# Routing the last group of a mixture-of-experts layer in two segments

## The chip, the cores and the metric

The kernel runs on one core of a Trainium2 chip. The metric is the device time of one execution in microseconds (us), and the smaller the better. A core has five engines that run side by side, each through its own queue of instructions in a fixed order: TensorE (PE, matrix products; PEld is its loading of weights), VectorE (DVE), ScalarE (ACT), GpSimd (POOL) and SyncE (SP). Transfers between the chip's main memory and the on-chip memory run on 16 DMA engines; an instruction on SP, ACT or POOL only issues one. An engine waits on semaphores: an instruction that waits holds up everything behind it in its queue.

## The reference

The program is a four-layer network on 2708 nodes with 256 features. Each layer adds a graph step and a feed-forward step to x. The change touches the feed-forward step of layer 1, a mixture of 8 experts in which each node goes to one:

```python
def _L1_ffn_ref(x, W1, b1, Wg, bg, Wd, bd):
    H = gelu(x @ W1 + b1)                      # 2708 x 1024
    probs = softmax(H @ Wg + bg)               # 2708 x 8
    assign = argmax(probs)
    for e in range(8):
        y = H @ Wd[e] + bd[e]                  # 1024 -> 256
        out = out + where(assign == e, probs[:, e] * y, 0)
```

All data are float32. How many nodes each expert gets depends on the data.

## The kernel before

**Tiles and groups.** The 2708 rows are 22 tiles of 128 rows (the last has 20). In layer 1 the graph step runs in three groups of tiles (GROUPS1): 0 to 7, 8 to 15 and 16 to 21. Once a group's graph step is done, `send1` works on its tiles: it normalizes them, makes the hidden rows H in pairs of tiles (L362 products, L364 Gelu on ACT), the gate's logits (L1085, L1092), turns H back into rows (L1102 on DVE) and writes it to a table `hid` in main memory (L1108, L1111; POOL issues these for the first two groups, ACT for the last one). After all pairs of the group come the softmax (ACT changes its function table for the exponential, then about a dozen short DVE instructions) and `route`.

**Routing.** `route` counts with products of the 0/1 choices (L389, L391), how many rows each expert has so far, and gives each row a place in a list `taken` (in main memory) that is sorted by expert within the group. `scatter` then writes one record (row number and probability) for each row, one POOL transfer for each tile (L497, taken). The records stand in a tile `names` with a single buffer; a POOL copy fills in the row numbers (L1115), so the copy for the next group has to wait until the scatters of the one before have read it.

**Blocks.** An expert's rows are worked on in blocks of 128. `blocks` computes on DVE, from the counts, for each block its expert (`b_ei`) and the places of its records (`b_ix`). After two groups 9 blocks can be sure to be full whatever the data (A blocks: 2048 rows in 8 experts leave at most 127 over in each); their list is made after group two. After the last group the rest is listed (B blocks), 21 at most, of which 15 always run (ALWAYS) and 6 stand in a branch that is taken only if the data need more than 24 blocks in all.

**One block.** `Units` runs the blocks as a pipeline. For each block POOL issues three indirect transfers: the gather of its 128 records (L511, names; call it the names gather), the gather of its 128 hidden rows of 4 KB each (L648, hs; the row gather), and at its end the scatter of its result (L497, given). SP issues the load of its expert's weights (L1025, wb, 1152 KB), whose address is read from `b_ei`. PE turns the rows (8 transposes, L659, call it the turn; two ACT copies L660 follow) and multiplies (L698, the product, 16 records in the trace for each block); DVE adds the bias and scales (L699, L700). There are three buffers for rows, three for weights and two for results. `more` fetches up to four names tiles and three row tiles ahead, so that a new row gather waits for a turn to free a buffer.

**Order.** Each engine's order is laid out when the program is built, by a scheduler that goes by dependencies and estimated times. It moves the hidden layer of the last group in between the A blocks' products: PE begins the A blocks when the graph step ends, at 933 us, and works on both until 1014.7. The B blocks follow. A transfer that reads rows which were scattered (`past`) waits for those scatters.

Of the kernel before, what the change touches and what calls it, by code (L numbers as in the profile page):

```python
# [8 lines left out]
F32 = mybir.dt.float32  # L9
# [3 lines left out]
ALU = mybir.AluOpType  # L13
AX = mybir.AxisListType

P = 128
N = 2708
D = 256
DC = D // P
E = 8  # L20
# [9 lines left out]
GROUPS1 = [range(0, 8), range(8, 16), range(16, NT)]  # L30
# [6 lines left out]
def rows(t):  # L37
    return min(P, N - t * P)
# [28 lines left out]
def adj_ffn4(ctx: ExitStack, tc: tile.TileContext, a: dict, out: bass.AP):  # L67
    nc = tc.nc
    v, s, g, te = nc.vector, nc.scalar, nc.gpsimd, nc.tensor
# [340 lines left out]
    def blocks(pool, brief, known, NB, B, name, done=None, full=False, least=0):  # L410
# [12 lines left out]
        vec = pool.tile([P, K, E], F32, name="b_vec", tag="b_vec" + name)  # L423
# [12 lines left out]
        rest = cnt  # L436
        if done is not None:
            rest = pool.tile([P, E], F32, name="b_rest")
# [6 lines left out]
        nb = pool.tile([P, E, 1], F32, name="b_nb")  # L445
# [9 lines left out]
        ei = pool.tile([P, NB], I32, name="b_ei", tag="b_ei" + name)  # L455
        v.tensor_scalar(ei, eb[:, :, 0], float(E - 1), None, op0=ALU.min)
        v.tensor_tensor(vec[:, 0, :], nb[:, :, 0], end, ALU.subtract)
        if done is not None:
            v.tensor_tensor(vec[:, 0, :], vec[:, 0, :], done, ALU.add)
        v.tensor_tensor(hot, eb.to_broadcast([P, NB, E]),  # L460
                        count[:, None, :E].to_broadcast([P, NB, E]), ALU.is_equal)
        part = brief.tile([P, NB, K, E], F32, name="b_part", tag="b_part" + name, bufs=1)
# [17 lines left out]
                            ALU.mult)  # L480
            v.tensor_tensor(ix if full and i == len(known) - 2 else row, row, step, ALU.add)
        if full:

            took = pool.tile([P, E], F32, name="b_took")
            v.tensor_scalar(took, vec[:, 0, :], float(NB), None, op0=ALU.add)
            v.scalar_tensor_tensor(took, took, 0.0, nb[:, :, 0], op0=ALU.max, op1=ALU.min)
            return ei, ix, took
        v.tensor_tensor(step, pos, of[:, :, K - 1 : K].to_broadcast([P, NB, M]), ALU.is_ge)
        v.scalar_tensor_tensor(ix, step, 1e7, row, op0=ALU.mult, op1=ALU.add)
# [2 lines left out]
    scattered = {}  # L492
# [126 lines left out]
    class Units(Blocks):  # L619
# [43 lines left out]
        def begin(self, items):  # L663
# [3 lines left out]
            self.rows_todo = len(items)  # L667
            self.more(False)

        def more(self, weights=True):  # L670
            while self.names_todo and len(self.named) + len(self.rows) < 4:
                self.fetch_names(self.names_todo.pop(0))
            while self.rows_todo and len(self.rows) < 3:
                self.fetch_rows()
                self.rows_todo -= 1
            while weights and self.todo and len(self.ahead) < 2:
                self.fetch(self.todo.pop(0))

        def run(self, pool, items, during=None):
            self.names_todo += items  # L680
            self.todo += items
            self.rows_todo += len(items)
            self.more()
            turned = self.turn(pool, self.rows[0][1])
            n = 0
            while self.rows:
                w2, hT = self.ahead.pop(0), turned
                m, _ = self.rows.pop(0)
                self.more()
                if during is not None:  # L690
                    during(n)
                n += 1
                if self.rows:
                    turned = self.turn(pool, self.rows[0][1])
                y = pool.tile([P, D], F32, name="ys", bufs=2)
                q = pools["psum"].tile([P, W], F32, name="yacc", bufs=2)[:, :D]
                for f in range(HC):
                    te.matmul(q, lhsT=hT[:, f, :], rhs=w2[:, f, :], start=(f == 0), stop=(f == HC - 1))  # L698
                v.tensor_tensor(y, q, w2[:, HC, :], ALU.add)  # L699
                v.tensor_scalar(y, y, m[:, 1:2], None, op0=ALU.mult)  # L700
                scatter(self.given, m[:, 0:1].bitcast(I32), y, self.given.shape[0] - 1, self.ok)
# [309 lines left out]
    held = sum(rows(t) for q in GROUPS1[:-1] for t in q)  # L1011
    NA, MOST = 9, (N - E) // P + E + 1
    assert NA <= -(-(held - E * (P - 1)) // P)
    ALWAYS = 15
    with ExitStack() as l1:
        tp = l1.enter_context(tc.tile_pool(name="t1", reuse_waits="tile", bufs=1))
        w1 = mat(tp, "L1_ffn_W1", 1024)
# [46 lines left out]
        def send1(tiles):  # L1064
# [7 lines left out]
            for i0 in range(0, G, 2):  # L1072
                own = [(i, (i - i0) * P, rows(tiles[i])) for i in range(i0, min(i0 + 2, G))]
                w = own[-1][1] + own[-1][2]
                xT = gt.tile([P, DC, 2 * P], F32, name="xT4", bufs=2)
                for i, k, r in own:
                    xn = work.tile([P, D], F32, name="xn")[:r]
                    norm_to(xn, tiles[i], i, st)
                    turn_to(xT[:, :, k : k + r], xn, r)
                hT = gt.tile([P, HC, 2 * P], F32, name="hT", bufs=1)  # L1080
                hidden(hT, xT, w1, lambda f: b1[:, f : f + 1], 0, w, HC)
                p = ps_tmp()
                for f in range(HC):
                    q = f % 4 * Q
                    te.matmul(p[q : q + Q, :w], lhsT=wg[:, f, :], rhs=hT[:, f, :w],  # L1085
                              start=(f < 4), stop=(f >= HC - 4), tile_position=(0, q))
                lT = gt.tile([P, 2 * P], F32, name="lT", bufs=1)
                s.copy(lT[:, :w], p[:, :w])
                p = ps_tmp()
                for i, k, r in own:  # L1090
                    o = p[:r, (i - i0) * E : (i - i0 + 1) * E]
                    te.matmul(o, lhsT=lT[:, k : k + r], rhs=fold[:, :E], start=True, stop=True)  # L1092
                    v.tensor_tensor(lg[:r, i, :], o, bg[:r], ALU.add)

                queue = s if tiles is GROUPS1[-1] else g
                for i, k, r in own:
                    h = gt.tile([P, P // Q, HC * Q], F32, name="hrow", bufs=2)
                    n = -(-r // Q)
                    if r < P:
                        v.memset(hT[:, :, k + r : k + n * Q], 0.0)  # L1100
                    for f in range(0, HC, 4):
                        v.transpose(h[:, :n, f * Q : (f + 4) * Q].rearrange("p b (f i) -> p f b i", i=Q),  # L1102
                                    hT[:, f : f + 4, k : k + n * Q].rearrange(
                                        "p f (b j) -> p f b j", j=Q))
                    for q in range(P // Q):
                        dst = hid[tiles[i] * P : tiles[i] * P + r, q * HC * Q : (q + 1) * HC * Q]
                        if r == P:
                            queue.dma_start(dst.rearrange("(b j) c -> j b c", j=Q),  # L1108
                                            h[q * Q : (q + 1) * Q])
                        else:  # L1110
                            queue.dma_start(dst, h[q * Q : q * Q + r, 0, :])  # L1111
# [17 lines left out]
        for tiles in GROUPS1:  # L1129
# [66 lines left out]
            if end:  # L1196
# [5 lines left out]
                hc = l1.enter_context(  # L1202
                    tc.tile_pool(name="c1", side="right", reuse_waits="tile", bufs=1))
                work1.more()
            send1(tiles)
            if tiles is GROUPS1[-2]:
                full = blocks(hw, gt, known, NA, P, "A", full=True)
        rest = blocks(hw, gt, known, MOST - NA, P, "B", done=full[2])
        too_many = count_left(hw, (rest[2], ALWAYS))
        gate.close()  # L1210
        past = list(scattered["taken1"])
        items = [(rest, b, past, taken[1], False) for b in range(ALWAYS)]
        more = [(rest, b, past, taken[1], False) for b in range(ALWAYS, MOST - NA)]
        left = []

        def beside(b):
# [693 lines left out]
```

## Time and profile before

| | us |
|---|---|
| median of 3 runs | 1943.4 (1940.89 to 1946.63) |
| profiled execution | 1943.77 |
| its span | 1941.9 |
| PE busy | 1830.7 (94%) |
| DVE, ACT, POOL busy | 1090.2, 666.7, 347.4 |
| A blocks, first turn to last product | 933.4 to 1014.7 |
| B blocks, first turn to last product | 1029.6 to 1102.35 |
| first instruction of layer 2 that needs the result (x on DVE) | 1111.9 |

Times are counted from the start of the span. A busy time is the sum over an engine's instructions; a PE that is busy is not necessarily at its peak. In a list of instructions each row has its start, its length, the engine, the line of the code, the operation, the tiles written and read, and in brackets how long the engine stood idle before it and what it seems to have waited for. In the stretches each engine has its busy time and its number of instructions.

### The profile page before, as it was taken

To read this page: it belongs to the slowest core of one execution; us is meant where nothing else is said; L and a number is where in the kernel's file an instruction comes from. 1 tells how busy PE (TensorE), PEld (TensorE's weight loads), DVE (VectorE), ACT (ScalarE), POOL (GpSimd) and SP (SyncE) were. 2 spreads that over 40 slices of the span, in tenths; PEclk is the share of its full clock that TensorE was granted. 3 is DMA by queue.
4 is the path that set the end of the run, shared out by engine and by line. 5 is a ranking of instruction groups with operands and counts; after the bars stand their busy time and mean duration, and the time that the engine had idled before them with its cause. 6 is when DMAs were issued, how large, how long until landed. Compare 5 with 4: busy or idle time off the path is not lost.

```text
span 1941.9 us, 25771 instructions
## 1 busy us (share of the span) xinstructions
PE 1830.7 (94%) x9441; PEld 1332.3 (69%) x9441; DVE 1090.2 (56%) x2463; ACT 666.7 (34%) x1527; POOL 347.4 (18%) x405
## 2 busy tenths in 40 slices
PE   7999989999999999999887699999899999999997
PEld 6888778888888888887676578888566632232343
DVE  6776862443334434354431265555355499899895
ACT  7868732222223203022222252222243551131232
POOL 1004263333331002213436300000000000000000
PEclk9999989999998999999898899999899999999998
DMA  8435476877764443636768620000101001000000
GB/s 272 137 111 156 121 272 244 346 303 290 296 257 132 146 148 109 159 105 137 237 224 282 242 60 1 1 1 1 44 1 33 18 1 23 23 14 25 23 17 15
DMA packets 90141, 243.93 MB, mean 126 GB/s; under 512 B 18160, under 2 KB 44824, under 8 KB 80793
## 3 DMA queue, kind: packets, MB, share of 16 engines
q1 hardware_dynamic: 70048, 197.09, 30.8%
q0 software_dynamic: 16960, 42.42, 6.9%
q10 hardware_dynamic: 3000, 2.70, 0.5%
q8 instruction: 77, 1.26, 0.3%
q14 instruction: 56, 0.45, 0.1%
HBM read 216.29 MB, written 28.71 MB: 126 GB/s over the span
## 4 chain that ended last, share of the span: by engine, by line
PE 74%; DMA 10%; DVE 7%; issue 4%; ACT 2%; POOL 1%; SPq 0%; POOLq 0%; DVEq 0%; ACTq 0%
PE num L1808 10%; PE ps_acc L1392 9%; PE acc L908 8%; PE ps_tmp L362 7%; PE acc L1189 7%; PE ps_acc L596 6%; PE yacc L606 5%; PE den L1818 5%; PE ps_tmp L255 4%; PE ps_acc L1575 3%; DMA given<-ys,xs 3%; PE yacc L698 2%; DMA hs<-hid,names 2%; DMA given<-ys,names 1%; DVE e L1778 1%
## 5 line engine op out<-in xcount | busy, mean ns | idle before, releaser
L1778 DVE SCALAR_TENSOR_TENSOR e<-arena,G,mask 128x1024 f32<-128x1024 f32 (+1 forms) x264 | 287.8, 1150 | 17.3 <-PE den L1818 17.3
L1808 PE MATMUL num<-e,wh 128*64 128x512 f32 (+4 forms) x1056 | 214.9, 551 | 0.3 <-ACT L_gnn_W L1235 0.3
L1392 PE MATMUL ps_acc<-hh,e 128*128 128x257 f32 x882 | 199.2, 382 | 1.7 <-ACT o L1337 1.7
L1189 PE MATMUL acc<-sup,adrow 128*128 128x256 f32 x882 | 198.9, 382 | 1.9 <-DVE adrow L1161 1.7
L908 PE MATMUL acc<-msg,wt 128*128 128x256 f32 x882 | 198.8, 382 | 1.8 <-DVE wt L866 1.2
L1189 PEld LDWEIGHTS acc<-sup,adrow 128*128 128x128 f32 x882 | 164.9, 190 | 29.2 <-issue 5.2
L908 PEld LDWEIGHTS acc<-msg,wt 128*128 128x128 f32 x882 | 165.8, 191 | 27.9 <-DVE wt L866 2.1
L1392 PEld LDWEIGHTS ps_acc<-hh,e 128*128 128x128 f32 x882 | 163.7, 190 | 29.3 <-ACT o L1337 4.7
L598 ACT ACTIVATE hTs<-ps_acc,wa 128x256 f32<-128x256 f32 (+1 forms) x192 | 88.8, 466 | 244.0 <-PE yacc L606 164.7
L596 PE MATMUL ps_acc<-xTs,wa 128*128 128x256 f32 (+1 forms) x768 | 170.5, 375 | 0.9 <-DVE xTs L569 0.8
L606 PE MATMUL yacc<-wb,hTs 128*128 128x256 f32 x736 | 167.4, 379 | 1.9 <-DVE ys L608 1.9
L596 PEld LDWEIGHTS ps_acc<-xTs,wa 128*128 128x128 f32 x768 | 137.7, 191 | 26.6 <-ACT hTs L598 3.4
L1808 PEld LDWEIGHTS num<-e,wh 128*64 128x64 f32 (+1 forms) x1056 | 66.2, 136 | 127.6 <-issue 107.4
L606 PEld LDWEIGHTS yacc<-wb,hTs 128*128 128x128 f32 x736 | 137.5, 190 | 20.1 <-DVE ys L608 2.5
L1386 DVE SCALAR_TENSOR_TENSOR e<-Rb,G,mask 128x640 f32<-128x640 f32 (+2 forms) x110 | 85.2, 775 | 92.7 <-PE ps_acc L1392 92.5
L1818 PE MATMUL den<-e,wh 128*32 128x512 f32 (+4 forms) x1056 | 118.0, 548 | 0.0
L1158 DVE TENSOR_SCALAR mask<-adrow 128x1024 uint8<-128x1024 f32 (+1 forms) x66 | 41.5, 628 | 123.4 <-DMA adrow<-in_adjT 123.1
L204 ACT COPY xT<-ps_tmp 128x256 f32<-128x256 f32 x98 | 34.1, 366 | 209.9 <-PE ps_tmp L203 200.9
L698 PE MATMUL yacc<-wb,hTs 128*128 128x256 f32 x384 | 94.0, 396 | 0.1
L866 DVE SCALAR_TENSOR_TENSOR wt<-adrow,wt 128x640 f32<-128x640 f32 (+3 forms) x67 | 71.1, 1063 | 29.6 <-ACT wt L141 29.3
L1818 PEld LDWEIGHTS den<-e,wh 128*32 128x32 f32 (+1 forms) x1056 | 30.2, 108 | 77.9 <-issue 73.8
L698 PEld LDWEIGHTS yacc<-wb,hTs 128*128 128x128 f32 x384 | 73.9, 199 | 11.1 <-issue 1.2
(448 smaller groups left out, 2603.1 us busy)
## 6 DMA issues: line engine op xcount, KB each, us to landing
adhalf<-in_adjT SPq DMA_DIRECT2D x42, 677.0 KB
wb<-in_L_ffn_W2p SPq DMA_DIRECT2D x24, 1152.0 KB
wb<-in_L_ffn_Wdp SPq DMA_DIRECT2D x24, 1152.0 KB
wa<-in_L_ffn_W1b SPq DMA_DIRECT2D x24, 1028.0 KB
adrow<-in_adjT SPq DMA_DIRECT2D x42, 512.0 KB
adrow<-in_adjT SPq DMA_DIRECT2D x42, 320.0 KB
adrow<-in_adjT SPq DMA_DIRECT2D x21, 576.0 KB
adrow<-in_adjT SPq DMA_DIRECT2D x21, 448.0 KB
```

The source lines that it names most:

```text
L362: te.matmul(p[:, :w], lhsT=w1[:, c, f * P : (f + 1) * P], rhs=xnT[:, c, c0 : c0 + w], start=(c == 0), stop=(c == DC - 1))
L596: te.matmul(p[:, f % 2, : m * P], lhsT=w1[:, c, f * P : (f + 1) * P], rhs=xT[:, c, : m * P], start=(c == 0), stop=(c == DC - 1))
L598: s.activation(hT[:, f, : m * P], p[:, f % 2, : m * P], AF.Gelu, bias=bias[:, f : f + 1])
L606: te.matmul(q[:, k, :], lhsT=hT[:, f, k * P : (k + 1) * P], rhs=w2[:, f, :], start=(f == 0), stop=(f == HC - 1))
L698: te.matmul(q, lhsT=hT[:, f, :], rhs=w2[:, f, :], start=(f == 0), stop=(f == HC - 1))
L908: te.matmul(p[:q, n - pair[0], :], lhsT=wt[:, k : k + q], rhs=msg[:r, j, :], start=(j == 0 and n == pair[0]), stop=(j == FULL - 1 and n == ...
L1189: te.matmul(p[:q, n - pair[0], :], lhsT=ad[:, k : k + q], rhs=sup[:r, j, :], start=(j == 0 and n == pair[0]), stop=(j == FULL - 1 and n == ...
L1386: v.scalar_tensor_tensor(e[:r, :w], Rb[:r, c0 : c0 + w], G[:r, j, :], mask[:r, j, c0 : c0 + w], op0=ALU.max, op1=ALU.mult)
L1392: te.matmul(p[:, : D + 1], lhsT=e[:, k : k + q], rhs=hh[:, j, :], start=(j == 0), stop=False)
L1778: v.scalar_tensor_tensor(e[:, :w], slow[:, m % 2, k, :w], G[:, j, 2 * pair + k, :], mask[:, j, c0 : c0 + w], op0=ALU.max, op1=ALU.mult)
L1808: te.matmul(num[k * DK : (k + 1) * DK, hf, :q], lhsT=wh[some, j, 2 * pair + k, :DK], rhs=e[some, h0 - c0 : h0 - c0 + q], start=(j == 0), s ...
L1818: te.matmul(den[z : z + Q, :q], lhsT=wh[some, i, 2 * pair + k, DK : DK + 1] .to_broadcast([some.stop - some.start, Q]), rhs=e[some, h0 - c ...
```

## The change

The last group is now sent in two parts: tiles 16 to 19, and tiles 20 and 21. After the first part there are 2560 rows routed, of which 13 full blocks are certain: 9 A blocks and 4 more (D blocks), which are listed and handed to the pipeline between the two parts. The B blocks are listed after the second part: 17 at most, 11 of them always run, and again 6 in the branch.

```diff
-    ALWAYS = 15
+    parts = GROUPS1[-1][:4], GROUPS1[-1][4:]
+    held2 = held + sum(rows(t) for t in parts[0])
+    ND = 4
+    assert NA + ND <= -(-(held2 - E * (P - 1)) // P)
+    ALWAYS = 11
...
-                queue = s if tiles is GROUPS1[-1] else g
+                queue = s if tiles[0] >= GROUPS1[-1][0] else g
...
-            send1(tiles)
+            send1(tiles if not end else parts[0])
             if tiles is GROUPS1[-2]:
                 full = blocks(hw, gt, known, NA, P, "A", full=True)
-        rest = blocks(hw, gt, known, MOST - NA, P, "B", done=full[2])
+        past = list(scattered["taken1"])
+        full = blocks(hw, gt, known, ND, P, "D", done=full[2], full=True)
+        work1.add([(full, b, past, taken[1][:held2], True) for b in range(ND)])
+        send1(parts[1])
+        rest = blocks(hw, gt, known, MOST - NA - ND, P, "B", done=full[2])
...
         items = [(rest, b, past, taken[1], False) for b in range(ALWAYS)]
-        more = [(rest, b, past, taken[1], False) for b in range(ALWAYS, MOST - NA)]
+        more = [(rest, b, past, taken[1], False) for b in range(ALWAYS, MOST - NA - ND)]
```

`add` is the first three lines of `run`, taken out so that it can be called before. In `blocks` the count of blocks that a full list takes from each expert (`took`) is computed earlier and adds what was done before, as the D list follows the A list:

```diff
         v.tensor_tensor(vec[:, 0, :], nb[:, :, 0], end, ALU.subtract)
+        if full:
+
+            took = pool.tile([P, E], F32, name="b_took", tag="b_took" + name)
+            v.tensor_scalar(took, vec[:, 0, :], float(NB), None, op0=ALU.add)
+            v.scalar_tensor_tensor(took, took, 0.0, nb[:, :, 0], op0=ALU.max, op1=ALU.min)
         if done is not None:
             v.tensor_tensor(vec[:, 0, :], vec[:, 0, :], done, ALU.add)
+            if full:
+                v.tensor_tensor(took, took, done, ALU.add)
```

The last group's softmax, routing and record scatters are thus done twice, for four tiles and for two, and ACT changes its function table twice more. In the built program POOL issues as many transfers as before; the D blocks' gathers stand before the record scatters of the second part. The order and number of SP's transfers are unchanged.

More of the change, by code (lines that the diff above doesn't have):

```diff
@@ L482, in blocks @@
         if full:
-            took = pool.tile([P, E], F32, name="b_took")
-            v.tensor_scalar(took, vec[:, 0, :], float(NB), None, op0=ALU.add)
-            v.scalar_tensor_tensor(took, took, 0.0, nb[:, :, 0], op0=ALU.max, op1=ALU.min)
             return ei, ix, took
@@ L668, in begin, with add @@
             self.more(False)
+        def add(self, items):
+            self.names_todo += items
+            self.todo += items
+            self.rows_todo += len(items)
         def more(self, weights=True):
@@ L679, in run @@
         def run(self, pool, items, during=None):
-            self.names_todo += items
-            self.todo += items
-            self.rows_todo += len(items)
+            self.add(items)
             self.more()
```

## The prediction

> **What bounds the kernel now.** I read the page first: PE is busy 94% of the span, so what the change can win is PE time lost somewhere. The span was then cut into stretches around the end of layer 1, where the change acts.
>
> ```profile
> 1000.00:1014.70 14.70, 14.70 (x61) 12.41 (x60) 8.98 (x40) 1.08 (x2) 9.42 (x11) 0.79 0.48 144
> 1014.70:1029.60 14.90, 0.00 (x0) 0.02 (x1) 2.11 (x6) 0.00 (x0) 9.10 (x10) 0.67 0.75 236
> 1029.60:1045.00 15.40, 15.39 (x78) 13.63 (x79) 3.15 (x9) 4.39 (x8) 11.22 (x12) 0.87 0.60 187
> 1045.00:1060.00 15.00, 14.44 (x82) 12.39 (x81) 2.33 (x6) 3.22 (x6) 8.98 (x9) 1.00 0.94 351
> 1075.00:1090.00 15.00, 12.93 (x72) 11.27 (x71) 2.08 (x7) 3.22 (x6) 7.16 (x8) 1.00 1.01 395
> ```
>
> Columns: length, then busy time of PE, PEld, DVE, ACT and POOL, the granted PE clock, DMA share, GB/s. PE does nothing at all for 14.9 us: the nine A blocks are through, and the first B block (B0) has no rows. Behind it PE is full at first, then the DMA engines are (0.94 to 1.01) and PE loses a little on every block. The timeline tells what the gap waits for:
>
> ```profile
> 994.55 1.28 ACT L135 ACT_TABLE_LOAD   x1 [5.44 <-DMA hid<-hrow]
> 1002.34 0.17 DVE L407 CAST r_ix<-r_at 128x6 int32<-128x6 f32 x1
> 1003.25 0.98 POOL L497 DMA_INDIRECT taken<-names,r_ix  x1 [5.52 <-issue]
> ...
> 1009.74 0.91 POOL L497 DMA_INDIRECT taken<-names,r_ix  x1 [0.30 <-issue]
> ...
> 1018.94 1.05 POOL L511 DMA_INDIRECT names<-taken,b_ix  x1 [0.30 <-DMA wb<-in_L_ffn_Wdp]
> ...
> 1023.50 1.07 POOL L648 DMA_INDIRECT hs<-hid,names  x1 [0.30 <-issue]
> ...
> 1029.61 1.94 PE L659 MATMUL ps_acc<-ident,hs 128*128 128x128 f32 x8 [14.91 <-DMA hs<-hid,names]
> ```
>
> The reader is to see a chain of transfers in series: gate and routing done at 1002.5, six record scatters on POOL's queue (one each 1.3 us), their landing, B0's names gather, its landing, B0's row gather, its landing. No engine is the limit; POOL's order and the latencies are. Their spread, over all of layer 1's names gathers, then over the row gathers of the B blocks:
>
> ```profile
> L511 POOL DMA_INDIRECT names<-taken,b_ix x24: 991/999/1468, 923.1 to 1076.7; - x24
> ...
> DMA to landing us min/median/max: 2.3/5.6/11.8
> ```
>
> ```profile
> L648 POOL DMA_INDIRECT hs<-hid,names x15: 991/1023/1072, 1023.5 to 1086.1; - x15
> ...
> DMA to landing us min/median/max: 4.4/6.6/10.1
> ```
>
> And the end of the stage, PE alone:
>
> ```profile
> 1094.01 1.04 PE L659 MATMUL ps_acc<-ident,hs 128*128 128x128 f32 x8
> 1094.89 7.46 PE L698 MATMUL yacc<-wb,hTs 128*128 128x256 f32 x32
> ```
>
> The last product ends at 1102.35. The 15 B blocks took 1102.35 - 1029.61 = 72.7 us, 4.85 each, where PE alone needs 4.33 (0.87 for the turn, 3.46 for the product: the usual steps of the chain of waits).
>
> **The change part by part.** Products stay 24 (384 records, 16 a block). Four of the 15 blocks behind the gap become D blocks, D0 to D3, which can run in it. What must be priced is when D0's and B0's rows arrive now. All orders below are the built program's, engine by engine.
>
> *First segment.* Its last logits stand at 978.33 as before. ACT finishes its eight hid issues at 981.3, then the new table load 1.28 and the exponential 0.25: 982.85. Up to r_m DVE needs 2.1 (996.38 to 998.47 before): 985.0. PE then routes with 2 + 8 records; 16 took 1.90 at full clock, so about 1.4: 986.5. From the scan to r_ix 1.15: 987.7. Four record scatters at 1.3, the last issued at 991.7. The copy that fills the names tile for the second segment now waits on POOL for their landing, and D0's names gather stands behind it. Landing takes 6.2 to 7.8 (915.72 to its end at 922.0; 1009.74 to 1017.5); I take 6.8: 998.5, with the copy 998.8. POOL owes nobody anything during this wait: the row gathers of all A blocks are issued before it.
>
> *POOL from there.* Two names gathers, then D0's row gather when its names are in. B0's own instance before took 4.56 (1018.94 to 1023.50), the median is 5.6: 1003.4 or 1004.4. Seven issues at 1.3 (it, and six gathers and scatters) give 1012.5 or 1013.5. Two record scatters for the second segment 2.6; D3's row gather and a scatter 2.6; four small loads 0.83 + 0.59 + 0.58 + 0.56 = 2.6; a scatter 1.3; two loads 1.2: B0's names gather at 1022.8 or 1023.8, after 1018.94 before. Its names 4.56 or 5.6, its rows 6.1 (1023.50 to 1029.61) or 6.6: B0's turn at 1033.5 or 1036.0. That is 4 to 6 us later than before.
>
> *Second segment.* Its indices must be ready at 1012.5. PE starts its hidden layer at 987.9 (983.85 before: routing 1.4, 0.7 of wait for r_m, two more steps of A's products, that are saved later). The Gelu needs a second new table load, which the six hidden matmuls and a turn behind it cover on PE. ACT's eight hid issues then run 995.8 to 1001.2 (5.4 as before), table and exponential to 1002.8, DVE 2.3, routing 0.95, DVE 1.15: 1007.5 with a wait for PE. Slack 5 us. If that is gone, every us goes into B0. The roughly 70 added short DVE instructions at 0.2 are in these chains; beyond them DVE has room (8.98 of 14.7 busy in its fullest stretch).
>
> *PE.* A's products end near 1008.7. D0's turn needs rows issued at 1003.4 plus 6.1: 1009.5, and the last A product stands behind it: 1013.8. Three more turns and products at 4.33: D2's product ends at 1026.8. PE then waits 7 to 9 us for B0 instead of 14.9. A late D0 is swallowed there, up to that length.
>
> *Behind B0.* Left are 12 products and 11 turns, against 15 and 15: 12 x 4.85 - 0.87 = 57.3. End at 1090.8 or 1093.3, 11.5 or 9.1 earlier than 1102.35. Bounds of the 57.3: at PE's rate 12 x 3.46 + 11 x 0.87 = 51.1; at the DMA-full rate of the last stretches (turns from 1055.09 to 1093.80, 8 in 38.7 us, 4.84) no more than what I have. The weight loads are 24 in the same order on SP, three ahead; D's expert numbers stand long before a buffer is free.
>
> *Elsewhere.* The took lines move up by some places in layers 0 and 1, and a few layer 0 activations change places; no count changes. Such an instruction is 0.16 to 0.5: I take 0, bounds plus or minus 1, covered by PE, which is full there.
>
> **Sum.** Middle of 11.5 and 9.1: 10.3. The profiled execution took 1943.77 (span 1941.9), the median is 1943.4: nothing between them. 1943.4 - 10.3 = 1933.1, so **1933**.
>
> Two rules beside this sum. The trace's table load is 1.28 and the next activation starts 0.02 after it. The Trainium skill (ScalarE: Activation LUTs, What ACT_TABLE_LOAD costs) has 2.66 for each switch, with a drain; by it the first segment would be 1.4 later and the time about 1934.5, and the other switch lies in the slack. For transfers issued by POOL, DMA: Bandwidth & Descriptors (Anatomy of one DMA) gives 2.0 us and the bytes over 436 GB/s, so 2.0 for names and 3.2 for rows, where the rows here have 5.6 and 6.6. By it B0's rows would be in before D2's product ends, and the time would be 1943.4 - (1102.35 - 1026.8 - 57.3) = 1925. The measurements decide.
>
> **The rivals.**
>
> *Transfers give most of it back.* For it: the DMA engines are at 0.94 to 1.01 from 1045 on, and blocks move what they moved. Against it: D's transfers fall into a time with room: 0.52 x 14.7 + 0.25 x 14.9 = 11.4 us free before 1029.6. If only half of it can be used, because D's gathers go one at a time, about 5.5 is won: 1938.
>
> *PE's own rate behind B0.* With fewer blocks the DMA engines may not fill: 51.1 in place of 57.3 gives 6 more: 1927. Against it: less is loaded ahead at 1033 than at 1029.6 before.
>
> *Slower: POOL's serial chain.* D's gathers stand before the second segment's record scatters, and POOL issues in order. Landings in series: the four record scatters, D0's names, B0's names, B0's rows. It decides once B0's turn is later than 1102.35 - 57.3 = 1045.0, 9 us after my later figure. With all four at their longest (10.1 for scatters, 11.8 for names, 10.1 for rows) it is 3.3 + 6.2 + 6.2 + 3.5 = 19 later: 1055, and the kernel ends at 1953. Half of that excess is the break-even. For it: the B gathers run in the fullest traffic. Against it: 998 to 1033 has no more than today's 0.5 to 0.75.
>
> *It does not do what it says.* Were D's blocks not full, the guarded blocks would run: 6 x 4.85 = 29 us more. Against it: 2560 rows in 8 experts hold at least (2560 - 8 x 127)/128, so 13 full blocks, 9 + 4; and the 384 records are 24 blocks, so the guard was not entered.
>
> **How the numbers follow.** Forecast 0.62; transfers 0.16; PE's rate 0.10; POOL's chain 0.11; the last 0.01. About 0.3%, 5.8 us, is what a measurement can tell from no change: 1937.6 to 1949.2. Faster: 0.59 of the forecast, 0.05 of the transfers, 0.10 of PE's rate: 0.74. Same: 0.03 + 0.11 = 0.14. Slower 0.12. The forecast with its own bounds is 1930 to 1937; the range goes from PE's rate, 1927, to where the transfers give nearly all back, 1942.
>
> **What would show it.** B0's turn (the eleventh of the row transposes from the end) at 1033 to 1036, with an idle time of 7 to 9 before it; D0's turn near 1010; the names copy at 998; two more ACT table loads; a last product near 1092; DMA share above 0.7 between 1000 and 1030. Wrong: a names gather for D0 behind 1003; PE idle over 12 us before B0; a block rate behind B0 over 5.2, or a wait in POOL's queue on a turn or product of PE.

## The result and the profile after

The changed kernel takes 1947.05 us (median of 18 runs, 1940.51 to 1955.07), the kernel before 1943.08 beside it (18 runs, 1936.12 to 1949.94): ratio 1.0024, 95% interval 1.0014 to 1.0035, so 4 us slower where 10 us less were forecast. The profiled execution is one of its shorter ones (1943.66, span 1941.2): what it shows is where the forecast gain went, and not the whole of the 4 us.

The stretches, with columns as in the prediction:

```profile
1000.00:1014.70 14.70, 12.41 (x72) 10.61 (x71) 7.72 (x38) 4.61 (x8) 9.14 (x9) 1.00 0.81 273
1014.70:1029.60 14.90, 12.54 (x69) 10.70 (x69) 5.77 (x23) 2.54 (x5) 9.92 (x13) 1.00 0.80 256
1029.60:1045.00 15.40, 5.84 (x26) 5.03 (x25) 3.92 (x12) 1.73 (x4) 8.02 (x9) 0.78 0.64 194
1045.00:1060.00 15.00, 11.50 (x54) 9.63 (x54) 1.91 (x6) 2.28 (x5) 7.99 (x9) 0.89 0.74 250
1075.00:1090.00 15.00, 14.02 (x78) 12.09 (x76) 2.56 (x6) 3.22 (x6) 8.22 (x9) 1.00 1.00 379
```

The stretch that was empty before, 1014.7 to 1029.6, now has 12.5 us of PE work: the D blocks run where they were meant to. But the two stretches behind it, which were full (15.39 and 14.44), now lack 9.6 and 3.5. The gap was not filled, it was moved behind the D blocks. The timeline tells what holds B0 now (D0's row gather, the second indices, D0's turn, the second record scatters, B's block indices, two small loads, the product of D2, then B0's names gather, row gather and turn, the product of D3 and B1's turn):

```profile
1004.99 0.99 POOL L651 DMA_INDIRECT hs<-hid,names  x1 [2.08 <-issue]
1009.98 0.17 DVE L407 CAST r_ix<-r_at 128x2 int32<-128x2 f32 x1
1012.76 1.06 PE L662 MATMUL ps_acc<-ident,hs 128*128 128x128 f32 x8 [1.07 <-DMA hs<-hid,names]
1016.18 1.02 POOL L500 DMA_INDIRECT taken<-names,r_ix  x1 [0.31 <-issue]
1017.51 0.93 POOL L500 DMA_INDIRECT taken<-names,r_ix  x1 [0.30 <-issue]
1019.87 0.18 DVE L492 SCALAR_TENSOR_TENSOR b_ix<-b_step,b_row 128x17 int32<-128x17 f32 x1
1025.32 0.58 POOL L121 DMA_DIRECT2D L_ffn_gamma<-in_L_ffn_gamma  x1 [0.41 <-DMA taken<-names,r_ix]
1028.64 0.55 POOL L121 DMA_DIRECT2D L_ffn_beta<-in_L_ffn_beta  x1 [2.74 <-DMA hs<-hid,names]
1029.49 1.05 POOL L514 DMA_INDIRECT names<-taken,b_ix  x1 [0.31 <-DVE ys L705]
1029.39 3.62 PE L704 MATMUL yacc<-wb,hTs 128*128 128x256 f32 x16
1038.18 1.05 POOL L651 DMA_INDIRECT hs<-hid,names  x1 [5.54 <-issue]
1042.57 1.94 PE L662 MATMUL ps_acc<-ident,hs 128*128 128x128 f32 x8 [9.56 <-DMA hs<-hid,names]
1044.30 5.62 PE L704 MATMUL yacc<-wb,hTs 128*128 128x256 f32 x16
1053.42 1.07 PE L662 MATMUL ps_acc<-ident,hs 128*128 128x128 f32 x8 [3.50 <-DMA hs<-hid,names]
```

B0's names gather goes at 1029.49, 10.6 later than before (1018.94). Its row gather goes 8.7 after that (4.56 before), its rows are in 4.4 later, and its turn is at 1042.57, 13.0 later than before: just the time of three blocks at PE's 4.33, and three products fewer are left behind it (12 in place of 15). PE stands idle 9.56 before B0, 3.50 before B1 and (in the same list) 2.23 before D3 and 1.07 before D0: 16.4 in place of 14.9, all of it for rows and none for weights. D3's product took 5.62 in place of 3.62, at a granted clock of 0.78 to 0.89; that cost nothing, since B1's rows came 3.50 later still. The end of the stage:

```profile
1096.13 7.07 PE L704 MATMUL yacc<-wb,hTs 128*128 128x256 f32 x32
```

The last product ends at 1103.20, before at 1102.35: 0.85 later. Twelve products and 11 turns took 60.6. In a second profile of the same kernel, of a longer execution (after_again below, 1949.64), B0's turn is at 1042.10 and the last product ends at 1106.96; PE waits there for weights as well (1.82 before D1's product, 0.99 later on).

### The profile page after: what moved, and what is told of

Read it like the earlier page. It is cut to its first block, busy times and chain, and to the rows that moved or that the text cites. A ratio compares the mean times of both kernels' runs of the same rounds, so it can differ in the third digit from the quotient of the medians.

```text
span 1941.2 us, 25857 instructions
## 1 busy us (share of the span) xinstructions
PE 1827.7 (94%) x9443; PEld 1326.6 (68%) x9443; DVE 1098.6 (57%) x2535; ACT 669.3 (34%) x1530; POOL 348.0 (18%) x406
## 4 chain that ended last, share of the span: by engine, by line
PE 74%; DMA 10%; DVE 7%; issue 4%; ACT 2%; POOL 1%; SPq 0%; ACTq 0%; POOLq 0%; DVEq 0%
PE num L1822 10%; PE ps_acc L1406 9%; PE acc L914 8%; PE ps_tmp L362 8%; PE acc L1199 7%; PE ps_acc L599 6%; PE yacc L609 6%; PE den L1832 5%; PE ps_tmp L255 4%; PE ps_acc L1589 3%; DMA given<-ys,xs 2%; DMA hs<-hid,names 2%; DMA given<-ys,names 2%; DVE e L1792 1%; DMA adrow<-in_adjT 1%
## 5 line engine op out<-in xcount | busy, mean ns | idle before, releaser
L609 PEld LDWEIGHTS yacc<-wb,hTs 128*128 128x128 f32 x736 | 137.5, 190 | 21.1 <-DVE ys L611 3.5
L611 DVE TENSOR_TENSOR ys<-yacc,wb 128x256 f32<-128x256 f32 x46 | 19.5, 424 | 110.7 <-PE yacc L609 110.6
```

The costliest lines, as they stand in the source:

```text
L609: te.matmul(q[:, k, :], lhsT=hT[:, f, k * P : (k + 1) * P], rhs=w2[:, f, :], start=(f == 0), stop=(f == HC - 1))
```

## The experiments

Three theories. **1:** POOL's order and the transfers in series set B0's start. **2:** the traffic on the DMA engines, mostly the expert weights, takes back what is gained. **3:** the second routing itself is what costs. Every kernel is measured against the kernel before on the same chip; the runs fell on chips on which that takes 1943 to 1944, and on others on which it takes 1954 to 1956, so ratios are to be compared. A ratio whose interval holds 1 can't be told from no change.

| kernel | us | before beside it | ratio (95%) |
|---|---|---|---|
| after_again (changed kernel) | 1946.83 | 1943.28 | 1.0012 (0.9999 to 1.0026) |
| a6 seven loads last | 1943.45 | 1943.28 | 1.0002 (0.9986 to 1.0019) |
| a7 and records first | 1943.35 | 1943.28 | 1.0003 (0.9986 to 1.0019) |
| a10 seven loads in the middle | 1942.51 | 1943.73 | 0.9994 (0.9983 to 1.0005) |
| b10 same, kernel before | 1946.31 | 1943.73 | 1.0012 (0.9998 to 1.0026) |
| a11 a10 and records first | 1943.29 | 1943.73 | 0.9999 (0.9986 to 1.0011) |
| a20 a10 and four ys buffers | 1943.22 | 1943.24 | 1.0004 (0.9992 to 1.0017) |
| b20 same, kernel before | 1945.06 | 1943.24 | 1.0011 (0.9996 to 1.0027) |
| a4 changed, no weight traffic | 1924.10 | 1943.28 | 0.9900 (0.9874 to 0.9926) |
| b4 before, no weight traffic | 1934.60 | 1943.73 | 0.9959 (0.9944 to 0.9975) |
| a1 six loads last | 1959.26 | 1953.89 | 1.0030 (1.0016 to 1.0045) |
| b1 same, kernel before | 1955.62 | 1953.89 | 1.0014 (1.0000 to 1.0027) |
| a3 split, no D blocks | 1959.21 | 1953.89 | 1.0038 (1.0021 to 1.0054) |
| a5 a1 and records first | 1958.87 | 1953.89 | 1.0035 (1.0020 to 1.0050) |
| a12 changed, no weights for blocks 9 to 12 | 1955.95 | 1955.91 | 0.9999 (0.9985 to 1.0013) |
| b12 before, the same | 1950.54 | 1955.91 | 0.9975 (0.9963 to 0.9988) |
| a14 a10 with two D blocks | 1960.78 | 1955.91 | 1.0023 (1.0007 to 1.0039) |
| a16 two D blocks | 1962.17 | 1955.91 | 1.0037 (1.0020 to 1.0053) |

**First round: loads, order, the split alone.** In the changed kernel two small loads for layer 2 stand ahead of B0's names gather. a1 puts all six of them behind the last certain scatter, b1 does so in the kernel before, a5 adds that the second record scatters go ahead of D2's and D3's row gathers, and a3 keeps the split but makes no D blocks (the three lines that list them and hand them over go as well). The edits are shortened here.

```diff
# a1, b1
-        wr = mat(tp, "L2_ffn_Wr", E)
+        late = scattered["given1"][23].name
+        wr = mat(tp, "L2_ffn_Wr", E, past=late)   # past: after(i, past); so too br, b1, b2, gamma, beta
# a5 too, in fetch_rows
+            if self.places[1] - 1 in (NA + 2, NA + 3):
+                after(i, scattered["taken1"][-1].name)
# a3
-    ND = 4
-    ALWAYS = 11
+    ND = 0
+    ALWAYS = 15
```

> The changed kernel, with layer 2's six small loads ordered behind layer 1's last certain scatter. Theory 1 (POOL's order and the landings in series set B0's start): nothing but the landing of the second segment's records (1025.03 in the changed kernel) stands ahead of B0's names gather, so it goes at 1025.3 to 1026 in place of 1029.49; B0's turn 3.5 to 4.2 earlier than 1042.57, the time 3.5 to 4.2 below the changed kernel: 1943 to 1943.6. Theory 2 (loaded DMA engines set it; what goes earlier lands later): the names and rows of B0 take as much longer, B0's turn stays at 1042 to 1043, the time at 1947 within 1. Theory 3 (the split's own second routing is the cost): no change either, 1947.

> The kernel before with the same six loads ordered the same way, as the control. Theory 1: in the kernel before the names gather of B0 waited for the landing of the record scatters, not for the loads, so B0's turn stays at 1029.6 within 1 and the time at 1943 within 1.5. Theory 2: the loads are small, the same.

> The last group is routed in two segments of four and two tiles, but no D block is made: 15 B blocks behind it, as before. This is the split alone. Theory 1 (D's gathers and scatters on POOL put the second segment's record scatters late): without them these two scatters go as soon as the second indices stand, at 1010 to 1012, land near 1018 to 1019, and B0's names gather is at 1019 to 1021 against 1018.94 before; the time is 0 to 2 above the kernel before. Theory 3 (the second softmax, routing, table loads and indices cost the time): B0's names gather is at 1025 or later, and the time is 6 or more above the kernel before. Theory 2: as the kernel before within 1.5.

> The changed kernel with both orders: layer 2's six small loads behind the last certain scatter, and the row gathers of D2 and D3 behind the second segment's two record scatters. Theory 1: record scatters at 1012.9 and 1014.2 in place of 1016.18 and 1017.51, landed by 1021.7; B0's names gather near 1022.8, 6.7 earlier than in the changed kernel, B0's turn near 1036; D2's and D3's rows come 2.6 later, into PE's idle time. Time 1940 to 1942. Theory 2: 1946 to 1948.

a1 and a5 missed: both stay above the kernel before (the changed kernel itself was not run on this chip). The trace of a1 shows why: with six of the loads moved, the multiplication of w_l, a seventh load, stands on VectorE in the middle of B's block indices. VectorE waited 8 us for w_l (9 in a5), the indices behind it came late, and POOL held B0's names gather for them:

```profile
1046.54 0.43 DVE L268 TENSOR_TENSOR o<-w_l,L_gnn_a_r 128x256 f32<-128x256 f32 x1 [7.98 <-DMA w_l<-in_L_gnn_WT]
1048.17 1.63 POOL L518 DMA_INDIRECT names<-taken,b_ix  x1 [9.50 <-DVE b_ix L496]
```

So these two say nothing on theory 1. a3 speaks for theory 3: without any D block the time is 5.3 above the kernel before (theory 3 had said 6 or more, theory 1 at most 2). The timelines of a3 (the first record scatter of the second part, B0's names gather, B0's turn) and of b1 on the same chip (the first of its six record scatters, then the same):

```profile
1024.28 0.97 POOL L500 DMA_INDIRECT taken<-names,r_ix  x1 [3.56 <-issue]
1035.73 1.09 POOL L514 DMA_INDIRECT names<-taken,b_ix  x1 [1.68 <-DMA given<-ys,names]
1045.40 1.94 PE L662 MATMUL ps_acc<-ident,hs 128*128 128x128 f32 x8 [16.81 <-DMA hs<-hid,names]
```

```profile
1011.87 0.98 POOL L501 DMA_INDIRECT taken<-names,r_ix  x1 [4.66 <-issue]
1025.86 1.03 POOL L515 DMA_INDIRECT names<-taken,b_ix  x1 [3.15 <-DMA taken<-names,r_ix]
1037.34 1.94 PE L663 MATMUL ps_acc<-ident,hs 128*128 128x128 f32 x8 [16.50 <-DMA hs<-hid,names]
```

With the split and nothing in the gap, the second part's scatters begin 12.4 later than b1's six, and B0's turn is 8.1 later, although no D gather stands ahead of it. On this chip the second indices come late enough to matter; in the changed kernel's first profile they came 20.0 behind the first ones (989.99 and 1009.98), here and in the other kernels of such a chip 22 to 28.

**Second round: all seven loads, no weights.** a6 moves w_l too, a7 adds the records' order to that, a4 takes the expert weights' traffic away.

```diff
# a6
+        after(g.dma_start(wa[:, :, :D], a["L3_gnn_WT"]...), late)
# a4, and b4 later
         def weights1(b, e):
+            if b > 2:
+                return wbs[b % 3]
```

> The changed kernel unaltered, as the reference for the two beside it on one chip. All theories: 2 to 7 above the kernel before. What it is to tell: whether the second segment's record scatters wait for POOL's queue or for their indices r_ix, and what the names gather of B0 waits for, on this chip.

> The changed kernel with all seven loads for the later layers (layer 2's six and the w_l of layer 3) behind the last certain scatter. In the run with only six of them moved, w_l's multiplication stood on VectorE ahead of B's block indices b_ix and held them for 8 us; here it stands behind them. Theory 1 (POOL's order): the names gather of B0 follows the landing of the second segment's records, 4 us earlier than in the changed kernel, and the time is 3 to 5 below it, within 2 of the kernel before. Theory 2 (transfers) and theory 3 (the second routing itself): as the changed kernel within 1.5.

> The same with the second segment's two record scatters ahead of the row gathers of D2 and D3. Theory 1: the record scatters go 1 to 3 us behind their indices in place of 6, the names gather of B0 is 6 to 9 earlier than in the changed kernel, B0's turn comes with under 4 us of PE idle before it, and the time is 6 to 9 below the changed kernel, 1 to 4 below the kernel before. Theory 3: the indices come too late for this to help; the scatters wait for r_ix as long as they waited for POOL, and the time stays within 2 of the changed kernel. Theory 2: 1.5 at most.

> The changed kernel, with layer 1's expert weights loaded for the first three blocks only; the later 21 blocks compute with these three tiles, so their 1152 KB each are not moved. Theory 2 (the weights' traffic makes B0's names and rows land late): names near 3.7 and rows near 4.4 (the shortest in the changed kernel's trace), in place of 8.7 and 4.4 to 9.6, so B0's turn is 8 or more earlier than in the changed kernel, and PE runs at its own rate of 4.33 a block behind it. Theory 1: the names gather of B0 still goes within 2 us of where it goes in the changed kernel, and B0's turn is still behind 7 us or more of PE idle.

Times in us from the first record scatter of the same trace, so that where layer 1 began doesn't matter, with the wait before B0:

| trace | B0's names gather | its row gather | B0's turn | PE idle before it | B0's turn to the last product's end |
|---|---|---|---|---|---|
| changed kernel | 38.6 | 47.2 | 51.6 | 9.6 | 60.6 |
| after_again | 37.2 | 44.3 | 48.8 | 8.1 | 64.9 |
| a6 | 33.7 | 38.3 | 46.8 | 5.4 | 55.9 |
| a7 | 30.3 | 38.8 | 47.7 | 3.9 | 54.2 |
| a10 | 31.0 | 37.1 | 45.9 | 5.8 | 59.2 |
| a11 | 29.4 | 38.1 | 46.9 | 3.8 | 60.1 |
| a20 | 33.8 | 40.9 | 45.3 | 2.0 | 65.6 |
| a4 | 34.2 | 37.8 | 42.2 | 4.1 | 52.9 |

a6 did ahead of B0 what theory 1 said (the names gather 3.5 to 4.9 earlier), and layer 1's last product ended 6.5 earlier than before. Its time is 3.4 below after_again, as theory 1 had said (3 to 5), though the intervals overlap, and only level with the kernel before. Its timeline (names gather, B0's turn, the last products, w_l's load, its use, layer 2's first transposes) shows where that went:

```profile
1026.91 1.04 POOL L518 DMA_INDIRECT names<-taken,b_ix  x1 [2.92 <-DMA taken<-names,r_ix]
1039.99 1.94 PE L666 MATMUL ps_acc<-ident,hs 128*128 128x128 f32 x8 [5.40 <-DMA hs<-hid,names]
1088.72 7.14 PE L708 MATMUL yacc<-wb,hTs 128*128 128x256 f32 x32 [1.41 <-DMA wb<-in_L_ffn_Wdp]
1105.94 0.72 POOL L1302 DMA_DIRECT2D w_l<-in_L_gnn_WT  x1
1112.69 0.42 DVE L268 TENSOR_TENSOR o<-w_l,L_gnn_a_r 128x256 f32<-128x256 f32 x1 [3.72 <-DMA w_l<-in_L_gnn_WT]
1114.65 1.18 PE L207 MATMUL ps_tmp<-ident,xn 128*128 128x128 f32 x4 [18.78 <-ACT xn L248]
```

The products end at 1095.86, but layer 2 begins at 1114.65 (1115.06 before). From the last product to there it now takes 18.8 in place of 12.7, and 3.72 of these 6.1 more are VectorE's wait for w_l. a7 got its record scatters and B0's names gather 3.4 earlier than a6, yet the names took 8.5 to land and B0's turn came no earlier: theory 1 in its simple form fell there.

a4 is another matter: 1.0 per cent below the kernel before, though it must be held against that kernel without the same traffic (b4 below). Its names gather goes 3.0 to 4.4 earlier than in the two traces of the changed kernel, and B0's turn 6.6 to 9.4 earlier with 4.09 of idle time, where theory 1 had said 2 and 7 or more. Its row gather follows the names gather after 3.6 us, and the rows are in 4.4 later. Names gathers and row gathers of 1010 to 1050 in the kernel before, in the changed kernel, and in a4 (instructions, then the landing over them):

```profile
L511 POOL DMA_INDIRECT names<-taken,b_ix x9: 992/1003/1050, 1018.9 to 1046.2; - x9
DMA to landing us min/median/max: 2.3/4.8/9.0
...
L648 POOL DMA_INDIRECT hs<-hid,names x7: 991/996/1072, 1023.5 to 1044.9; - x7
DMA to landing us min/median/max: 4.4/6.0/10.1
```

```profile
L514 POOL DMA_INDIRECT names<-taken,b_ix x6: 991/1013/1050, 1010.3 to 1049.2; - x6
DMA to landing us min/median/max: 4.3/6.3/10.4
...
L651 POOL DMA_INDIRECT hs<-hid,names x5: 990/1048/2173, 1013.7 to 1047.8; - x5
DMA to landing us min/median/max: 4.2/8.8/11.1
```

```profile
L514 POOL DMA_INDIRECT names<-taken,b_ix x9: 992/997/1052, 1021.0 to 1049.7; - x9
DMA to landing us min/median/max: 2.2/3.2/3.5
...
L651 POOL DMA_INDIRECT hs<-hid,names x9: 991/1032/1802, 1008.7 to 1048.4; - x9
DMA to landing us min/median/max: 3.2/4.3/5.8
```

The middle numbers are the medians: 4.8 and 6.0 before, 6.3 and 8.8 with the change, 3.2 and 4.3 without the weights, over few gathers each. The mean DMA share of this stretch is 0.72, 0.76 and 0.45: between the first two kernels it hardly differs, so the share alone does not explain the longer landings of the second.

**Third round: the loads in the middle, and b4.** a10 puts the seven loads behind the 18th certain scatter and w_l's multiplication behind the sums that open layer 2 (`after(i, added)` in score_columns); b10 is the kernel before with the same, a11 is a10 with a7's order.

> The changed kernel with the seven loads for later layers put behind the scatter of the 18th of the 24 certain blocks, in the middle of the B blocks, and w_l's multiplication on VectorE behind the sums that open layer 2. In the run with the seven loads behind the last scatter, the last product of layer 1 ended at 1095.87, 6.5 earlier than in the kernel before, but layer 2 began no earlier: the tail then waited for these loads, which stood between the last scatters and the reads. Theory 1 (what POOL's queue holds back decides, at B0 and again at the tail): the last product still ends 5 to 7 earlier than before, layer 2's first transposes too, and the time is 4 to 7 below the kernel before (ratio 0.9965 to 0.998). Rival (the end of layer 1 is set by something else than its products): layer 2 begins as before and the ratio stays at 1.000 within 0.001.

> The kernel before with the same two edits, as the control. Theory 1: B0's names gather waits there for the six record scatters and not for the loads, so the time is the kernel before's within 2 (ratio 0.999 to 1.001). If the loads alone are the gain: as far below as the kernel beside it.

> As the first of these, with the second segment's two record scatters ahead of the row gathers of D2 and D3. Theory 1 in its simple form (the earlier the record scatters, the better) gives 1 to 3 more. In the pair without the middle place, the names gather of B0 came 3 earlier by it, but its names took 8.5 to land and D3's rows came late; if that repeats, no gain over the first, within 1.5.

> The kernel before, with layer 1's expert weights loaded for the first three blocks only; later blocks compute with these three tiles. The changed kernel without this traffic was 1.0 per cent (19 us) below the kernel before. Theory 2 (it is the traffic that eats the change's gain): 8 to 12 above that, ratio 0.994 to 0.997. Theory 1 (the gain is lost to order on POOL, with or without traffic): within 4 of it, ratio 0.988 to 0.992.

a10 comes out level with the kernel before, where theory 1 had said 4 to 7 below it. It is 3.8 below its own control b10 (1942.51, 1946.31), but the two intervals overlap. With these loads among the B blocks, these take 59.2 in place of a6's 55.9. In these traces the loads cost wherever they were put, while in the kernel before they were issued from 1010.6 to 1022.4, shortly before PE's gap and in it; one trace of each kernel is little to go by. a11 confirms a7: names gather 1.6 earlier, B0's turn not.

The pair a4 and b4 decides for theory 2 on the faster chips: b4 lies 10.5 above a4, where theory 2 had said 8 to 12 and theory 1 at most 4. Timelines: B0's names gather, row gather and turn and the last products of a4; then B0's turn and the last products of b4:

```profile
1021.00 1.05 POOL L514 DMA_INDIRECT names<-taken,b_ix  x1 [0.30 <-issue]
1024.59 1.05 POOL L651 DMA_INDIRECT hs<-hid,names  x1 [0.44 <-issue]
1028.94 1.94 PE L662 MATMUL ps_acc<-ident,hs 128*128 128x128 f32 x8 [4.09 <-DMA hs<-hid,names]
1074.75 7.07 PE L704 MATMUL yacc<-wb,hTs 128*128 128x256 f32 x32
```

```profile
1022.51 1.94 PE L659 MATMUL ps_acc<-ident,hs 128*128 128x128 f32 x8 [13.22 <-DMA hs<-hid,names]
1083.09 7.07 PE L698 MATMUL yacc<-wb,hTs 128*128 128x256 f32 x32
```

Without this traffic the change puts B0's turn 6.4 later, ends the last product 8.3 earlier (1081.82 and 1090.16), and the medians differ by 10.5 (1924.10 of four runs, 1934.60 of ten, on two chips on which the kernel before takes 1943.28 and 1943.73; the two intervals don't meet). That is about the gain that was forecast, 10.3, and it disappears when the weights are moved. The second routing is in a4 too, with its indices 20.0 behind the first as in the changed kernel, so on these chips theory 3 by itself is not what takes the gain.

The traces also tell where the traffic costs, as far as one of each kernel and two of the changed one go. From the first record scatter to B0's turn it adds 4.2 to the kernel before (26.4 and 22.2) and 6.6 to 9.4 to the changed one; from B0's turn to the last product's end it adds 5.1 to the kernel before (72.7 and 67.6) and 7.7 to 12.0 to the changed one. The gain is lost in both stretches, ahead of B0 and behind it.

**Fourth round: which weights, and a smaller fill.** a12 and b12 leave out only the weights of blocks 9 to 12 (`if 9 <= b <= 12` in weights1). a14 and a16 have ND = 2 and ALWAYS = 13, a14 on top of a10.

> The changed kernel without the weight loads of blocks 9 to 12 (these compute with the tiles of blocks 6 to 8). Traffic ahead of B0: B0's names and rows land in 10 to 11 together in place of 13.1, its turn comes 4 to 6 earlier against the first record scatter (46 to 47.5 in place of 51.6 in the changed kernel), and the time is 8 or more below the run beside it. Traffic behind B0: B0's turn stays within 2 of where it was, and the time is within 4 of the run beside it.

> The kernel before without the weight loads of blocks 9 to 12, which are its first four B blocks: the same bytes left out. B0's turn stays within 2 of before; the first B blocks run at PE's rate, so the time is 1 to 4 below the kernel before. It is the number that the run beside it is measured against.

> Two D blocks and 13 certain B blocks in place of four and 11, with the seven loads in the middle of the B blocks. The second segment's record scatters stand behind two row gathers in place of three, and half of the D weights are loaded ahead of B0. If queue and traffic ahead of B0 are the cost: B0's turn 4 to 6 earlier than with four D blocks and the same loads (1039.97), one block's length of gap left, layer 1's end at 1094 to 1097, the time 2 to 5 below that run (1942.5): ratio 0.997 to 0.999. If the fill is all that counts: two blocks less in the gap, 3 to 6 above it.

> Two D blocks and 13 certain B blocks, nothing else altered in the changed kernel. If queue and traffic ahead of B0 are the cost: 2 to 6 below the changed kernel, ratio to the kernel before 0.999 to 1.001. If the fill is all that counts: 3 or more above the changed kernel, ratio 1.003 or more.

This was on the chips with 1954 to 1956. a12 is 5.4 above b12, not 8 below it: on such a chip the D blocks' own weights are not what takes the gain, or not alone. In a12's trace B0's turn comes 50.1 behind the first record scatter (1054.62, 1004.50), with 3.23 of idle time before it; the second indices were at 1030.62, 27.1 behind the first. Two D blocks gain nothing either (1.0023 and 1.0037). The changed kernel itself was not run on this chip, so that four and two D blocks, or a12 and the same with all weights, are not compared directly.

**Fifth round: late read-out.** Theory 4: a product that is read out late holds its weight tile, so the next weights come late. In the changed kernel the products of D0 and D1 end at 1021.6 and 1026.3, and VectorE reads them out at 1028.81 and 1040.57: there are two ys buffers, and before the first of these read-outs VectorE waited 8.76 for the scatter of an earlier result. (The expectation below counts these blocks one too high.) Four buffers (`bufs=4`), with a10's edits, in both kernels:

> The changed kernel with the seven loads in the middle of the B blocks, and four ys buffers in place of two. Theory 4 (late read-out holds the weight tiles): D1's to D3's products are read out within 1 us of their end, so the weights of B0 to B2 go 5 to 10 earlier than at 1030.41, 1031.33 and 1040.57 (the run with two buffers); the DMA share between the first indices and B0's turn rises, the B blocks run at 4.5 to 4.8 in place of 5.0, and the time is 3 to 6 below that run's 1942.5: ratio 0.996 to 0.998. Theory 2 (traffic ahead of B0 lengthens the landings): the weights go earlier, but B0's names and rows land as much later; ratio 0.999 to 1.001.

> The kernel before with the same loads moved and four ys buffers, the control. Theory 4: the last A products are read out earlier, but nothing waits for them in the 14.9 us gap; in the B blocks, where the DMA engines are full, an earlier weight load gives little: ratio 0.999 to 1.002, as with two buffers (1.0012). If the buffers themselves are the gain: as far below as the run beside it.

The read-out of D0 to D2 came at once (1017.37, 1022.69, 1031.27 in a20), the next weights were issued at 1017.83, 1023.14 and 1031.72, and PE waited only 1.95 before B0. No time was gained: the B blocks took 65.6 in place of 59.2, with waits for rows as below (B0's turn, B2's turn, the last turn and the last two products):

```profile
1033.18 1.07 PE L668 MATMUL ps_acc<-ident,hs 128*128 128x128 f32 x8 [1.95 <-DMA hs<-hid,names]
1046.22 1.06 PE L668 MATMUL ps_acc<-ident,hs 128*128 128x128 f32 x8 [2.21 <-DMA hs<-hid,names]
1088.41 1.94 PE L668 MATMUL ps_acc<-ident,hs 128*128 128x128 f32 x8 [4.23 <-DMA hs<-hid,names]
1090.15 8.61 PE L710 MATMUL yacc<-wb,hTs 128*128 128x256 f32 x32
```

Theory 4 fell. Of the kernels that do all the work, none beats the kernel before by more than its interval.

## Why the prediction was wrong

Point by point, on the profiled execution:

- *First segment.* Nearly right. The first indices came at 989.99 in place of 987.7, since ACT's hid issues ended at 983.87 and not at 981.3; the names copy at 999.71 (998.8), D0's row gather at 1004.99 (1003.4 or 1004.4).
- *POOL from there.* This step failed: "B0's names gather at 1022.8 or 1023.8" was 1029.49. POOL was 0.9 late at the names copy, 2.7 to 3.7 at the second record scatters (1016.18; 1012.5 or 1013.5) and 5.7 to 6.7 at B0's names gather. The largest part, 3.0, arose behind the record scatters, where the loads were priced by their issue times alone, 2.6 and 1.2. In fact gamma stood 0.41 until the records had landed, 7.5 after the last issue, and beta another 2.74 until an earlier gather's rows were in. a6 measures it: without the loads the names gather is 3.5 to 4.9 earlier.
- *The landings, in the same step.* The names at 4.56 or 5.6 and the rows at 6.1 or 6.6, so 10.7 to 12.2 together, were 13.1; all of the excess and more lay in the names (8.7), while the rows took 4.4, less than priced. Durations and medians of the kernel before were taken for a stretch whose DMA share the change itself raises from 0.48 and 0.75 to 0.81 and 0.80. POOL 5.7 to 6.7 late and the landings 0.9 to 2.4 beyond that: B0's turn at 1042.57 in place of 1033.5 or 1036.0.
- *PE.* D0's turn was at 1012.76 (1009.5), and D2's product ended at 1033.0 (1026.8), after waits of 1.07 and 2.23 for rows. So the idle time before B0, 9.56 where 7 to 9 were forecast, is nearly right by luck: B0 and the D blocks ahead of it were late together.
- *Behind B0.* 57.3 was 60.6; B1 alone waited 3.50 for its rows, 11.1 after their issue. (The turn that the prediction reads at 1093.80 is at 1094.01, so its rate is 4.87 and not 4.84; this changes nothing.) The 7.8 from the middle of the forecast's turn and these 3.3 are the 11.1 between 10.3 earlier and 0.85 later.
- *Second segment.* Indices at 1009.98 (1007.5), within the slack on this chip; on the other it was not within it. Left out was the chain on VectorE from them to B's block indices: 9.9 here (1009.98 to 1019.87), as before. Before, six record scatters and their landing hid it; now two have to, and in this trace they still did (the names gather went at 1029.49).
- *The rivals.* "Transfers give most of it back" had the mechanism, as a4 and b4 show, and too small a price: it gave back half, and all of it went. The argument against it, that "D's transfers fall into a time with room", was the error: 0.19 to 0.36 of the DMA engines' time stayed free from 1000 to 1045, and B0's names and rows took 13.1 all the same. "POOL's serial chain" decides from 1045.0, it was said; B0's turn stayed 2.4 short of that and the time was lost all the same, since the 57.3 didn't hold.
- *The signs.* D0's turn, the names copy, the added table loads and the DMA share came about as forecast, and three signs of being wrong stayed away (D0's names gather at 1000.53, PE idle 9.56, 5.12 a block): their bounds were too wide to tell. The fourth, a wait of POOL for a turn, came (3.15 at 1054.63), but it stands in the kernel before too (3.08 at 1051.59).

By the Trainium skill (DMA: Bandwidth & Descriptors, Anatomy of one DMA) the prediction's estimate was 2.0 us for names and 3.2 for rows. The traces don't agree: a4, without the weights' traffic, has medians of 3.2 and 4.3, and the changed kernel 6.3 and 8.8.

Shown: that the gap moved behind the D blocks; that loads on POOL hold B0's names gather by about 4; that on the faster chips the change is worth about its forecast without the weights' traffic, and that this traffic takes it back both ahead of B0 and behind it. Open: by which path. a7, a11 and a20 each removed one wait ahead of B0 and found it again, in a landing or in the B blocks. The three row buffers may have a part in it, which is not shown: at 4.33 a block they leave about 13 us from a turn to the next one on the same buffer, and row landings from 1030 to 1092 had a median of 8.6 and a longest of 11.1 in the changed kernel (7.0 and 10.1 before, 4.3 and 4.5 in a4), with POOL's queue to pass ahead of them. More row buffers were not tried. Open too is how much theory 3 adds on the slower chips, where a3 alone costs 5.3: a4 and b4 were not run there, nor a3 on the faster ones.

## What to carry to other kernels

A gap on one engine is not free room on the others: look at what the queues and the DMA engines do in it, because the work that goes in displaces them and meets longer landings. Price a transfer by rows from a stretch with the traffic that there will be after the change, and a small load on a queue by what it has to wait for, not by its issue time. Leaving out the heavy traffic in both kernels tells, in one pair of runs, whether the plan fails by itself or by that traffic.

## What had not been expected of the hardware

The landing of a small gather grew with the traffic though the DMA engines were not full: names gathers had medians of 3.2 without the weights at DMA shares of 0.39 to 0.54, and 6.3 with them at 0.64 to 0.81. A load whose data nobody needs yet can hold POOL's queue: beta waited 2.74 for the landing of a row gather (D3's, whose turn began at 1028.49), whose data it doesn't use, and 2.91 in the second profile. That gather stands eight transfers before beta in POOL's order both times; why this holds beta is not shown. And the chips seem to differ in more than speed: with the kernel before only 0.6 per cent apart (1943 and 1954 to 1956), the second indices came 20 us behind the first in every profile on the one kind and 22 to 28 on the other; no kernel with the split was profiled on both.
